# A four-layer gated model in one kernel: key constants and dispatch tables prepared beside an attention, slots in four stages, a shorter pipeline of product keys

## The chip, the core and the metric

One core of a Trainium2 chip runs the kernel. The metric is the device time of one execution in microseconds; lower is better. The engines are TensorE (PE: matmuls and transposes; its weight loads appear as PEld), VectorE (DVE), ScalarE (ACT), GpSimd (POOL), and SyncE (SP), which here only issues DMA transfers. Each engine works through its own list of instructions in order.

## The reference

Sixteen blocks of 128 tokens with 256 features pass through four layers. Each layer adds a gated cross-attention to a context and a gated feed-forward part:

```python
for l in range(4):
    x = x + tanh(g_xattn[l]) * attention[l](layernorm(x), ctx, ctx)
    x = x + tanh(g_ffn[l]) * ffn[l](layernorm(x))
# ffn[0]: top-1 of 8 experts; ffn[1]: top-2 of 8 experts and a shared one
# ffn[2]: soft mixture, 64 experts of 32 slots
logits = (x @ phi_w.T + phi_b).reshape(t, z, 64, 32)
D, C = softmax(logits, axis=3), softmax(logits, axis=2)
X = clip(einsum('tznp,tzd->npd', D, x), -33000, 65000)
Y = tanh(layernorm(X)) @ expert_w + expert_b
y = einsum('tznp,npH->tzH', C, Y)
# ffn[3]: product keys, 8 heads, two halves of 32 keys
q = batchnorm(x @ Wq + bq)              # over all tokens
s0, s1 = l2norm(q[..., :32]) @ l2norm(sub_key0).T, l2norm(q[..., 32:]) @ l2norm(sub_key1).T
# top 4 of each half, softmax over the 16 sums as weights w on experts idx
y = (gelu(expert_down[idx] @ x) * w) @ expert_up[idx]
```

## The kernel before

The residual x stays in SBUF as 16 tiles of 128 by 256. The stages run one after the other: attention 0, its experts, attention 1, its experts (routing, the shared expert, then sorted blocks), attention 2, the soft mixture (dispatch, slots, combine), attention 3, the product keys. Weights come through a pool `wp` of four large slots; normalised and transposed activations through `xtp` of four; PSUM has eight banks, each handed out by `bank`. Blocks under `manual_schedule` keep the order in which the code issues them on the named engines; elsewhere a scheduler orders the instructions when the kernel is built. In both cases each engine's order is fixed before the run, and SP's queue issues its transfers in order. A tile that takes space which a closed pool held waits until the old tiles' users, DMAs included, are done.

The experts end with POOL's scatter of each block's rows to `results` in DRAM (L974). Attention 2 (`xattn16`, L417) clears the gaps of three value tiles (L434), makes the keys of all four groups in its opening (`keys`, L442, 32 matmuls at L448, ACT adds the bias into `kraw` at L451), fetches the scattered rows (`fetch`, L508: `got`) and adds them to x (`add_gated`, L265), normalises and transposes x (L200 to L247), projects queries (L467) and values (L493), and then goes block by block: scores (L538), maxima, exponentials (L572), sums, transposes (L591), values, output. Near its end each block is normalised once more for the feed-forward part (`k`, `xnT`). An argument `draining`, used by another layer, is called in each step t.

The soft mixture, `attention_ffn2` (L1231), loads `phi` and its bias `phib`. `dispatch(u)` (L1378) handles block b and half hf, u = hf*16 + b, 1024 of the 2048 slots: four matmuls into two banks (L1386), bias added by DVE (`lg`, L1389), spilled to DRAM for the combine (L1390), maximum over the 32 slots of an expert (`red`, L1393), subtraction (L1396), exponential (ACT, L1397), maximum over experts (`top`, L1398), sum (L1400), reciprocal (L1401), and the multiply of d by POOL (L1402). `gather` (L1405) multiplies d with the normalised block into accumulators (L1412), two steps behind. After the first half, the slots 0 to 3 (groups of eight experts) run inside the second half's steps, each in three stages three steps apart in start: gather with norm (transposes, clip, statistics, `rs` on POOL by L200 and L201, `nm` on DVE at L1286, tanh on ACT at L1288), turn (transposes at L1297), expert (matmuls at L1308, with `ew` weights). Slots 4 to 7 come behind the last step, in an order written out by hand with the first shifts (L1348), sums (L1359 to L1362) and scalings (L1366 to L1369) of the combine. The combine then turns each block's weights and multiplies with the slots' outputs (L1492).

The product keys, `attention_ffn3` (L1521), start with the constants: `par` and `key` are loaded (L1528), POOL builds `havg`, `blk`, `half` and clears `kd` (L1532 to L1557), DVE squares and sums the keys, `inv_norm` (L1545) takes the power on POOL, then DVE's max and reciprocal, four scalings into the block-diagonal `kd` (L1560), and PE turns it to `kdT` (L1563). In the order as built these fall among the last slots, and the turn of kd just before attention 3's keys (L293). After attention 3 the queries' mean and variance over all tokens are taken; ACT does the gelu rows (`activations`, L1613); then a software pipeline over blocks runs stages with lags: square, norms and products, root, `exps` (L1703), `best_four` (sixteen MAX8 at L1711 and MATCH_REPLACE8 at L1715), `weigh` (L1720 to L1738; the product `pr` on POOL), `mix` (PE, L1751 and L1755), weight (L1760), turn, project (L1771), leave.

## Time and profile before

| what | us |
|---|---|
| runs of the kernel before | 1973.61, 1974.9, 1976.91 |
| median | 1974.9 |
| the profiled execution | 1977.58 |
| its span in the profile | 1975.9 |

The stages lie in that span about like this (from the timeline, by the first and last instruction of each):

| stage | from | to |
|---|---|---|
| attention 0 and experts 0 | 0 | 369 |
| attention 1 and experts 1 | 369 | 862 |
| attention 2 | 862 | 1021 |
| dispatch, with slots 0 to 3 | 1021 | 1274 |
| slots 4 to 7 | 1274 | 1306 |
| combine | 1306 | 1451 |
| attention 3 | 1451 | 1792 |
| product keys | 1792 | 1976 |

A timeline line gives start, busy time, engine, line of the code, operation, output<-inputs, shapes and how often; in brackets the idle time of that engine before it and what ended it. PE's order is fixed, so a bracket on a PE line tells what the whole engine stood waiting for. All times are of one profiled execution.

### The profile page before, as it was taken

To read this page: it belongs to the slowest core of one execution; us is meant where nothing else is said; L and a number is where in the kernel's file an instruction comes from. 1 tells how busy PE (TensorE), PEld (TensorE's weight loads), DVE (VectorE), ACT (ScalarE), POOL (GpSimd) and SP (SyncE) were. 2 spreads that over 40 slices of the span, in tenths; PEclk is the share of its full clock that TensorE was granted. 3 is DMA by queue.
4 is the path that set the end of the run, shared out by engine and by line. 5 is a ranking of instruction groups with operands and counts; after the bars stand their busy time and mean duration, and the time that the engine had idled before them with its cause. 6 is when DMAs were issued, how large, how long until landed. Compare 5 with 4: busy or idle time off the path is not lost.

```text
span 1975.9 us, 31036 instructions
## 1 busy us (share of the span) xinstructions
PE 1824.1 (92%) x10345; PEld 1219.4 (62%) x10345; DVE 1250.5 (63%) x3715; ACT 924.7 (47%) x3047; POOL 807.7 (41%) x972
## 2 busy tenths in 40 slices
PE   7996999978889999999989989889999999999897
PEld 4774566556646666656754434368866777775776
DVE  4885222389762222249969999989927667673797
ACT  5993222399931222239951121244524434443874
POOL 5873332377510454448832222211002222230796
PEclk9997999999999999999999999989999999999899
DMA  5002787510000788861012424543200000000000
GB/s 168 15 18 90 287 300 276 160 34 26 18 23 26 264 315 318 304 201 34 2 45 84 185 102 170 203 175 128 86 1 1 1 1 1 23 1 1 7 17 22
DMA packets 53138, 204.21 MB, mean 103 GB/s; under 512 B 11760, under 2 KB 31728, under 8 KB 42224
## 3 DMA queue, kind: packets, MB, share of 16 engines
q0 software_dynamic: 13584, 117.32, 16.3%
q1 hardware_dynamic: 38752, 84.87, 12.2%
q8 instruction: 84, 1.38, 0.3%
q14 instruction: 78, 0.64, 0.1%
q10 hardware_dynamic: 640, 0.00, 0.0%
HBM read 171.75 MB, written 30.41 MB: 102 GB/s over the span
## 4 chain that ended last, share of the span: by engine, by line
PE 39%; DVE 17%; ACT 4%; issue 3%; POOL 2%; DMA 2%; POOLq 0%; SPq 0%; ACTq 0%; DVEq 0%
PE pg L938 6%; PE po L1492 4%; PE pd L969 3%; PE pk L293 3%; PE pq L305 3%; PE po L388 3%; PE pv L316 3%; ACT e L572 2%; DVE rep L1715 2%; PE av L378 2%; PE sc L335 2%; DVE d L1396 2%; DVE tot L1400 1%; DVE red L1393 1%; PE pe L364 1%
## 5 line engine op out<-in xcount | busy, mean ns | idle before, releaser
L938 PE MATMUL pg<-we,xT 128*128 128x512 f32 (+1 forms) x520 | 238.4, 588 | 0.6 <-ACT xT L217 0.6
L585 POOL TENSOR_TENSOR e<-e,sums 128x512 f32<-128x512 f32 x192 | 199.0, 1069 | 69.6 <-DVE sums L582 33.2
L944 DVE TENSOR_TENSOR h<-sg,pg 128x256 f32<-128x256 f32 x132 | 54.3, 411 | 226.1 <-ACT sg L943 226.1
L572 ACT ACTIVATE e<-sc,mx 128x128 f32<-128x128 f32 x512 | 181.6, 421 | 15.9 <-DVE mx L550 14.8
L943 ACT ACTIVATE sg<-pg 128x256 f32<-128x256 f32 x132 | 49.7, 376 | 279.4 <-PE pg L938 278.1
L356 POOL TENSOR_TENSOR e<-e,rec 128x512 f32<-128x512 f32 x64 | 65.3, 1041 | 228.1 <-DVE rec L355 145.4
L938 PEld LDWEIGHTS pg<-we,xT 128*128 128x128 f32 x520 | 94.3, 193 | 78.8 <-issue 70.6
L904 POOL DMA_INDIRECT we<-in_we,rows x54 | 51.8, 958 | 213.7 <-PE pd L969 151.7
L572 ACT ACTIVATION_READ_ACCUMULATOR e<-sc,mx 128x1 f32 x512 | 133.1, 260 | 0.0
L1402 POOL TENSOR_TENSOR d<-d,tot 128x1024 f32<-128x1024 f32 x32 | 62.7, 1959 | 169.9 <-DVE tot L1401 153.2
L1412 PE MATMUL acc<-d,k 128*128 128x512 f32 x256 | 122.4, 620 | 9.5 <-POOL d L1402 9.3
L591 PE MATMUL pe<-ident,e 128*128 128x128 f32 x768 | 104.2, 278 | 28.6 <-DVE mx L555 14.2
L969 PE MATMUL pd<-we,hT 128*128 128x256 f32 x520 | 125.3, 383 | 1.2 <-ACT hT L958 1.2
L1397 ACT ACTIVATE d<-d 128x1024 f32<-128x1024 f32 x32 | 33.8, 1057 | 195.6 <-DVE d L1396 183.1
L969 PEld LDWEIGHTS pd<-we,hT 128*128 128x128 f32 x520 | 96.9, 190 | 39.2 <-issue 22.9
L1492 PE MATMUL po<-yt,cT 128*128 128x256 f32 x512 | 120.9, 380 | 0.0
L1386 PE MATMUL pl<-phi,xnT 128*128 128x512 f32 x256 | 117.5, 604 | 0.0
L200 POOL TENSOR_SCALAR ve<-mv 128x1 f32<-128x1 f32 (+1 forms) x136 | 30.5, 225 | 208.6 <-DVE mv L207 174.4
L591 PEld LDWEIGHTS pe<-ident,e 128*128 128x128 f32 x768 | 85.7, 141 | 47.4 <-POOL e L585 24.1
L572 ACT ACTIVATE e<-e,mx 128x128 f32<-128x128 f32 x256 | 99.2, 402 | 1.2 <-DVE mx L555 1.2
L1492 PEld LDWEIGHTS po<-yt,cT 128*128 128x128 f32 x512 | 92.4, 190 | 10.1
L1412 PEld LDWEIGHTS acc<-d,k 128*128 128x128 f32 x256 | 48.8, 198 | 73.1 <-issue 53.5
(315 smaller groups left out, 4360.9 us busy)
## 6 DMA issues: line engine op xcount, KB each, us to landing
spill<-lg SPq DMA_DIRECT2D x32, 512.0 KB, 3.0
ew<-in_ew SPq DMA_DIRECT2D x8, 2048.0 KB, 10.0
cw<-spill SPq DMA_DIRECT2D x14, 1024.0 KB, 8.3
got<-results SPq DMA_DIRECT2D x48, 128.0 KB, 2.1
normed<-xn SPq DMA_DIRECT2D x32, 128.0 KB, 1.7
aw<-in_aw SPq DMA_DIRECT2D x6, 512.0 KB, 3.8
ws<-in_we SPq DMA_DIRECT2D x2, 1536.0 KB, 6.6
we<-in_we SPq DMA_DIRECT2D x1, 2176.0 KB
```

What stands on the lines that cost most here:

```text
L293: nc.tensor.matmul(pk, lhsT=wk[:, k, c * P : (c + 1) * P], rhs=ctxT[g][:, k, :], start=(k == 0), stop=(k == 1))
L305: nc.tensor.matmul(pq[:, i * gt : (i + 1) * gt], lhsT=wq[:, k, (c + i) * P : (c + i + 1) * P], rhs=xnTs[g][:, k, :], start=(k == 0), stop= ...
L356: nc.gpsimd.tensor_tensor(e, e, rec.unsqueeze(2).to_broadcast([P, 4, S]), ALU.mult)
L572: nc.scalar.activation(e[:, c, :], sc[:, c, :], AF.Exp, bias=mx[:, h : h + 1], scale=sign, accum_out=sums[b][:, h : h + 1],)
L585: nc.gpsimd.tensor_tensor(e, e, r, ALU.mult)
L591: nc.tensor.transpose(pe[:, c * P : (c + 1) * P], e[:, c, :], ident)
L938: nc.tensor.matmul(pg[:, 0 : 2 * m].rearrange("p (g i) -> p g i", g=2), lhsT=tokens[j][:, k, :], rhs=wgu[:, k, :, i0 : i0 + m], start=(k = ...
L969: nc.tensor.matmul(pd[:, 0:D], lhsT=hT[0:m, ic, :], rhs=wd[0:m, ic, :], start=(ic == 0), stop=(ic == nic - 1))
L1386: nc.tensor.matmul(pl, lhsT=xnT[b // 4][:, k, tok], rhs=phi[:, k, n], start=(k == 0), stop=(k == 1))
L1402: nc.gpsimd.tensor_tensor(dv, dv, tot.unsqueeze(2).to_broadcast([P, 32, 32]), ALU.mult)
L1412: nc.tensor.matmul(acc[hf][k][q], lhsT=keep[b][:, k * P : (k + 1) * P], rhs=d[:, q * 512 : (q + 1) * 512], start=(b == 0), stop=(b == B - 1),)
L1492: nc.tensor.matmul(pos[b][:, 0:D], lhsT=cT[:, c, :], rhs=yt[2 * q + c // 2][:, c % 2, :], start=(q == 0 and c == 0), stop=(q == 3 and c == 3),
```

## The change

Seven edits, in the order of the code.

1. The constants of the product keys move, unchanged, into a function that is called at the start of the soft mixture, ahead of attention 2; their pool stays open to the end.
2. `phi` and `phib` are loaded into two of the four weight slots during attention 2 (step 2), and the first dispatch step's logits are issued in its step 21, in the tail. `phib` loses its own tile.
3. The slots in the loop have four stages, one step apart (gather, squash, turn, expert), with four `xs` buffers. As the tables hold two weight slots, expert weights are loaded two ahead and then one behind each expert; the last three are issued at the dispatch's end.
4. In the last dispatch step the multiply of d is DVE's, and `top` comes behind it.
5. The last slots are in another order; the shift and the exponentials of combine block 2 move a few steps back into the combine.
6. The product keys' stages have smaller lags, with `exps` last in a step, four gelu rows a step, and one step fewer in all. The last block's product is split between POOL (3 of 8 heads) and DVE.
7. The mask bias of attention 3 uses the `row` pool's tiles.

```diff
+def key_constants():
+    pkc = ctx.enter_context(tc.tile_pool(name="pkc", bufs=1))
+    par = pkc.tile([P, 6], F32, name="par")
+    nc.sync.dma_start(out=par, in_=a["par3"])
+    key = pkc.tile([P, 32], F32, name="key")
+    nc.sync.dma_start(out=key, in_=a["keys3"])
...
+    kdT = pkc.tile([P, P], F32, name="kdT")
+    pt = bank("pt")
+    nc.tensor.transpose(pt[:, 0:P], kd, ident)
+    nc.scalar.copy(kdT, pt[:, 0:P])
+    return par, havg, blk, kdT
...
+        constants = key_constants()
         kept = es.enter_context(ExitStack())
         kp = kept.enter_context(tc.tile_pool(name="keep", bufs=1))
         keep = [kp.tile([P, D], F32, tag=f"k{b}", name=f"k{b}") for b in range(B)]
         norm, xnT = norm_stage(keep)
-        attention2((norm, None, None, None), joining)
+        tables, first = [], {}
+        def logits(u, q):
+            hf, b = divmod(u, B)
+            n = slice(hf * 1024 + q * 512, hf * 1024 + (q + 1) * 512)
+            pl = bank("pl")
+            for k in range(2):
+                nc.tensor.matmul(
+                    pl, lhsT=xnT[b // 4][:, k, (b % 4) * S : (b % 4 + 1) * S], rhs=tables[0][:, k, n],
+                    start=(k == 0), stop=(k == 1),
+                )
+            return pl
+        def draining(t):
+            if t == 2:
+                t = load_slot(a["phi"], 4096, "phi")
+                tables.append(t[:, 0:4096].rearrange("p (c n) -> p c n", c=2))
+                pb = wp.tile([P, WSLOT], F32, tag="w", name="phib")[:, 0:2048]
+                nc.sync.dma_start(out=pb, in_=broadcast(a["phib"], 2048))
+                tables.append(pb)
+            if t == B + 5:
+                for q in range(2):
+                    first[q] = logits(0, q)
+        attention2((norm, None, None, None), joining, draining)
+        pb = tables[1]
         yp = es.enter_context(tc.tile_pool(name="soft", bufs=1))
-        pb = yp.tile([P, 2048], F32, name="phib")
-        nc.sync.dma_start(out=pb, in_=broadcast(a["phib"], 2048))
-        phi = load_slot(a["phi"], 4096, "phi")[:, 0:4096].rearrange("p (c n) -> p c n", c=2)
...
         def slots_gather(n, dp):
-            if 0 < n < 6:
-                load_experts(n + 2)
...
-            t = dp.tile([P, 2, D], F32, tag="xs", name="xs", bufs=2)
+            t = dp.tile([P, 2, D], F32, tag="xs", name="xs", bufs=4)
...
-        def slots_norm(n, dp):
-            slots_gather(n, dp)
-            slots_squash(n, dp)
-        slots = (slots_norm, slots_turn, slots_expert)
+        slots = (slots_gather, slots_squash, slots_turn, slots_expert)
...
             def dispatch(u):
                 hf, b = divmod(u, B)
                 lg = dp.tile([P, 1024], F32, tag="lg", name="lg", bufs=2)
-                tok = slice((b % 4) * S, (b % 4 + 1) * S)
                 for q in range(2):
                     n = slice(hf * 1024 + q * 512, hf * 1024 + (q + 1) * 512)
-                    pl = bank("pl")
-                    for k in range(2):
-                        nc.tensor.matmul(
-                            pl, lhsT=xnT[b // 4][:, k, tok], rhs=phi[:, k, n], start=(k == 0), stop=(k == 1)
-                        )
+                    pl = first.pop(q) if u == 0 else logits(u, q)
...
-                nc.vector.tensor_reduce(top[:, b, hf, :], lv.rearrange("t n p -> t p n"), AX.X, ALU.max)
+                if u < 2 * B - 1:
+                    nc.vector.tensor_reduce(top[:, b, hf, :], lv.rearrange("t n p -> t p n"), AX.X, ALU.max)
                 tot = dp.tile([P, 32], F32, tag="tot", name="tot")
                 nc.vector.tensor_reduce(tot, dv, AX.X, ALU.add)
                 nc.vector.reciprocal(tot, tot)
-                nc.gpsimd.tensor_tensor(dv, dv, tot.unsqueeze(2).to_broadcast([P, 32, 32]), ALU.mult)
+                if u < 2 * B - 1:
+                    nc.gpsimd.tensor_tensor(dv, dv, tot.unsqueeze(2).to_broadcast([P, 32, 32]), ALU.mult)
+                else:
+                    nc.vector.tensor_tensor(dv, dv, tot.unsqueeze(2).to_broadcast([P, 32, 32]), ALU.mult)
+                    nc.vector.tensor_reduce(top[:, b, hf, :], lv.rearrange("t n p -> t p n"), AX.X, ALU.max)
...
-                    if t in (12, 13, 14):
-                        load_experts(t - 12)
-                    n, i = divmod(t - B - 2, 3)
-                    if 0 <= n < 4:
-                        slots[i](n, dp)
+                    if t in (12, 14):
+                        load_experts((t - 12) // 2)
+                    for i, stage in enumerate(slots):
+                        n, late = divmod(t - B - 2 - i, 3)
+                        if late == 0 and 0 <= n < 4:
+                            stage(n, dp)
                     if t >= 2:
                         gather(t - 2)
+                    n, late = divmod(t - B - 6, 3)
+                    if late == 0 and 0 <= n < 3:
+                        load_experts(n + 2)
...
                 dispatch(2 * B - 1)
+                load_experts(5)
                 fetch_early(1)
+                load_experts(6)
+                load_experts(7)
                 gather(2 * B - 3)
                 gather(2 * B - 2)
...
                 combine_sum(0, dp)
-                for n in (4, 5):
-                    slots_gather(n, dp)
-                for n in (4, 5):
-                    slots_squash(n, dp)
-                combine_scale(0)
+                slots_gather(4, dp)
+                slots_gather(5, dp)
+                slots_squash(4, dp)
+                slots_gather(6, dp)
+                slots_squash(5, dp)
                 slots_turn(4, dp)
-                slots_gather(6, dp)
+                slots_gather(7, dp)
+                slots_squash(6, dp)
                 slots_turn(5, dp)
-                slots_gather(7, dp)
                 slots_expert(4, dp)
                 fetch(1)
-                for n in (6, 7):
-                    slots_squash(n, dp)
+                slots_squash(7, dp)
+                slots_turn(6, dp)
+                combine_scale(0)
                 slots_expert(5, dp)
-                for n in (6, 7):
-                    slots_turn(n, dp)
-                for n in (6, 7):
-                    slots_expert(n, dp)
+                slots_turn(7, dp)
+                slots_expert(6, dp)
+                slots_expert(7, dp)
...
+                    if u == 4:
+                        for i in range(3):
+                            combine_exp(2, i)
                     if q == 0 and b + 1 < B:
                         combine_exp(b + 1, 3)
-                    if q > 0 and b + 2 < B:
+                    if q > 0 and 0 < b < B - 2:
                         combine_exp(b + 2, q - 1)
                     if 0 <= u - 2 < 4 * B:
                         spread(u - 2)
-                    if q == 0 and b + 2 < B:
+                    if q == 0 and 0 < b < B - 2:
                         combine_shift(b + 2)
                     if q == 1 and b + 1 < B:
                         combine_sum(b + 1, cp)
                     if q == 2 and b + 1 < B:
                         combine_scale(b + 1)
+                    if u == 3:
+                        combine_shift(2)
...
+def attention_ffn3(constants):
     norm, xnT = norm_stage()
     with ExitStack() as es:
+        par, havg, blk, kdT = constants
         cp = es.enter_context(tc.tile_pool(name="pkc", bufs=1))
-        par = cp.tile([P, 6], F32, name="par")
...
-        activations(7)
...
-            rn = norms.pop(b)
+            rn, sc = norms.pop(b), raw.pop(b)
             w = pp.tile([P, 16, 32], F32, tag="wgt", name="wgt")
             for h in range(16):
-                nc.scalar.activation(w[:, h, :], raw[b][:, h, 0:32], AF.Exp, scale=rn[:, h : h + 1])
-            found[b] = w
+                nc.scalar.activation(w[:, h, :], sc[:, h, 0:32], AF.Exp, scale=rn[:, h : h + 1])
+            found[b] = w, replaced.pop(b)
         def best_four(b):
-            sc = raw.pop(b)
+            sc = raw[b]
...
-                pr, w0.unsqueeze(3).to_broadcast([P, 8, 8, 32]),
-                wv[:, :, 1, :].unsqueeze(2).to_broadcast([P, 8, 8, 32]), ALU.mult,
-            )
+            for engine, h in ((nc.gpsimd, slice(0, 8)),) if b < B - 1 else (
+                (nc.gpsimd, slice(0, 3)), (nc.vector, slice(3, 8))
+            ):
+                n = h.stop - h.start
+                engine.tensor_tensor(
+                    pr[:, h], w0[:, h].unsqueeze(3).to_broadcast([P, n, 8, 32]),
+                    wv[:, h, 1, :].unsqueeze(2).to_broadcast([P, n, 8, 32]), ALU.mult,
+                )
...
-            (2, root), (6, weight), (3, exps), (7, leave), (4, weigh), (1, norm_sums), (1, products),
-            (6, turn), (3, best_four), (5, mix), (6, project), (0, square),
+            (2, root), (5, weight), (6, leave), (3, weigh), (1, norm_sums), (1, products),
+            (5, turn), (2, best_four), (4, mix), (5, project), (0, square), (2, exps),
         )
-        for t in range(B + 7):
-            activations(min(B, 7 + 3 * (t + 1)))
+        for t in range(B + 6):
             for lag, stage in stages:
+                if stage == exps:
+                    activations(min(B, 4 + 4 * (t + 1)))
...
-            mf = rp.tile([P, S], F32, tag="mf", name="mf", bufs=2)
+            mf = row.tile([P, D], F32, tag="xn", name="mf")[:, 0:S]
...
-def attention2(after, joining):
+def attention2(after, joining, draining):
     load_attention(2)
-    xattn16(2, after=after, joining=joining)
-attention_ffn2(attention_ffn1(attention_ffn0()))
-attention_ffn3()
+    xattn16(2, after=after, joining=joining, draining=draining)
+attention_ffn3(attention_ffn2(attention_ffn1(attention_ffn0())))
```

In the first block the middle, left out, is the code of L1531 to L1560 as it was. The order as built: kdT's transpose stands on PE between the experts' last matmuls (L969) and attention 2's keys (L448); on DVE the key work stands among the first additions of `got`; on POOL the memsets, selects and the power stand behind the last scatter (L974), mixed with the value tiles' memsets; on SP's queue, phi's load (with no change of place), then par and key, then the first reads of `got`, with phib between two of them. In the dispatch's second half DVE's order around a slot becomes aggregate, reciprocal, one lg addition, `nm`, where it was aggregate, `nm`, reciprocal for slots 1 to 3.

## The prediction

> **What bounds the kernel now.** The page's busy shares come first: TensorE (PE) looks like the limit, but the share is a mean over stages, and the chain that ended last gives DVE 17% as well. So I read the stages that the change touches, each in the answer for stretches of time (columns: length, then busy time and instruction count of PE, PEld, DVE, ACT, POOL, then granted clock, DMA share, GB/s).
>
> ```profile
> PE 1824.1 (92%) x10345; PEld 1219.4 (62%) x10345; DVE 1250.5 (63%) x3715; ACT 924.7 (47%) x3047; POOL 807.7 (41%) x972
> PE 39%; DVE 17%; ACT 4%; issue 3%; POOL 2%; DMA 2%; POOLq 0%; SPq 0%; ACTq 0%; DVEq 0%
> ```
> ```profile
> 900.00:1000.00 100.00, 95.42 (x972) 73.80 (x973) 90.90 (x192) 95.62 (x467) 84.08 (x112) 1.00 0.05 15
> 1050.00:1250.00 200.00, 192.29 (x543) 83.97 (x541) 183.55 (x209) 36.15 (x42) 54.07 (x34) 0.98 0.39 149
> 1510.00:1760.00 250.00, 250.00 (x1638) 179.82 (x1638) 170.24 (x366) 104.41 (x193) 65.55 (x91) 1.00 0.02 5
> 1850.00:1950.00 100.00, 90.37 (x498) 77.66 (x498) 95.38 (x732) 75.02 (x281) 94.19 (x51) 0.97 0.05 16
> ```
>
> Attention 2 (second 900 to 1000) has PE and ACT both at 95 of 100: nothing there can win back a late start. The dispatch (1050 to 1250) goes at DVE's pace, 7.27 us a step. Attention 3 is PE without a gap. The product keys (1850 to 1950) run at 7.7 us a block with DVE and POOL both full. So at each border a late start is carried to the end, and so is an early one.
>
> **Key constants ahead of attention 2's keys: +14.5 us (10.7 to 17).** The instruction order of the changed kernel puts the transpose of the scaled keys (kdT) on PE behind the last down-projections of the experts and ahead of the 32 matmuls of attention 2's keys (L448). In the timeline of before these 32 start with no gap:
>
> ```profile
> 861.69 13.90 PE L448 MATMUL pk<-ctxT,aw 128*128 128x512 f32 x32
> 862.59 0.97 POOL L974 DMA_INDIRECT results<-y,target  x1 [1.20 <-DVE y L973]
> 869.74 0.49 POOL L434 MEMSET v<- 128x128 f32 x3 [6.18 <-DMA results<-y,target]
> 871.99 0.48 DVE L265 SCALAR_TENSOR_TENSOR x<-got,wt,x 128x256 f32<-128x256 f32 x1 [9.68 <-DMA got<-results]
> 876.22 0.41 PE L243 MATMUL pt<-ident,xn 128*128 128x128 f32 x2 [0.63 <-DVE xn L232]
> ```
>
> The experts' last scattered row block, issued at 862.59, lands at about 869.65; the v memsets wait for it because their space was the experts'. The matmuls covered that wait. In the changed kernel the new tiles (par, key, havg, kd) take space from the same closed pools, so their loads and memsets can't start before 869.7, and everything on the way to kdT comes after: key is issued behind par on SP's queue at about 870.1 and lands 1.8 us later (the key load's time to landing in before), 871.9; k2 and its sum are two DVE instructions of 0.17, 872.3; the power on POOL stands behind the memsets and selects of havg, blk, kd (2.2 us, the block at 1282.2 to 1284.4 in before) and three v memsets of 0.17, so at 872.5, 0.6 long; max and reciprocal 0.15 each, between them two L265 of 0.48 whose rows have arrived; four scalings of 0.23 to 0.26: 875.6; PE's transpose 0.27, plus semaphores: the key matmuls start at about 876.2 instead of 861.69. That is 14.5 us in which PE stands.
>
> Behind the waiting transpose stand the key matmuls, then the transposes of x, the queries, and the first scores at 882.01. Two corrections. PE was idle 6.3 of the 30 us from 870 to 900 (a ramp that waits for normed rows); the rows will be ready during the stall: from the end of the key matmuls to the first scores the 6.4 us (875.6 to 882.0) shrink to the instructions themselves, about 4.7 us (two transposes 0.41, copy 0.37, queries 1.97, values 1.03, semaphores). Against that the clock: after a PE gap, instructions run at half rate for a while. At 1276.80, after 3.1 us of idle, eight acc matmuls took 5.30 us where full speed is 3.60; at 1039.93, after 4.8 us, 5.97. So +1.7 to +2.4 here, and I take 2.2: 14.5 − 1.7 + 2.2 = 15.0, rounded down to +14.5 as some ramp idle after 882 (6.3 less what lies before it, 3.8 at most) may also go. That 3.8 in full is the lower bound, 10.7; another microsecond of landing and doubled clock loss is the upper, 17. Nothing is gained in return at the old place but 0.27 us of PE (1450.6, where PE is full, so it counts): −0.4 with its semaphore.
>
> **First dispatch logits inside attention 2's tail: −5.7 us (−6 to −3).** In before the dispatch starts like this:
>
> ```profile
> 1021.42 0.66 PE L243 MATMUL pt<-ident,k 128*128 128x128 f32 x2 [2.49 <-DVE k L232]
> 1025.59 0.69 DVE L1389 TENSOR_TENSOR lg<-pl,phib 128x512 f32<-128x512 f32 x1 [4.32 <-PE pl L1386]
> 1028.30 0.69 DVE L1389 TENSOR_TENSOR lg<-pl,phib 128x512 f32<-128x512 f32 x1 [2.01 <-PE pl L1386]
> 1029.02 1.22 DVE L1393 TENSOR_REDUCE red<-lg 128x32 f32<-128x1024 f32 x1
> ```
>
> DVE, which sets the pace, waits 4.32 + 2.01 us while four matmul pairs run at half clock (0.85 us each). In the changed kernel the first four stand between the transposes of blocks 14 and 15, where PE idles (2.49 before 1021.42): from 1018.95 at 0.43 a pass, done by 1022.4. The two additions then run at 1021.35 and 1022.65 and the maximum starts at 1023.35 instead of 1029.02. If their clock is still halved they end 3 us later: −3. The tables phi and phib now land in weight slots during attention 2, at a DMA share of 0.05, with 100 us to spare. On SP's queue phib stands among the reads of results; it lands long before use.
>
> **Slots in four stages inside the loop: +3.6 us (−2.5 to +6).** Look at what a shared port does to a tiny instruction:
>
> ```profile
> 1167.97 1.91 POOL L1402 TENSOR_TENSOR d<-d,tot 128x1024 f32<-128x1024 f32 x1
> 1168.04 1.86 DVE L1286 SCALAR_TENSOR_TENSOR nm<-mv,rs 128x2 f32<-128x2 f32 x1 [0.32 <-POOL rs L201]
> ```
> ```profile
> 1195.04 0.15 DVE L1286 SCALAR_TENSOR_TENSOR nm<-mv,rs 128x2 f32<-128x2 f32 x1
> 1196.19 1.92 POOL L1402 TENSOR_TENSOR d<-d,tot 128x1024 f32<-128x1024 f32 x1 [1.72 <-DVE tot L1401]
> ```
>
> nm has two elements a partition; 0.15 us when it runs before POOL's multiply of d, 1.86 when it comes 0.07 after it. In before this happens to slot 0 only, for slots 1 to 3 the order on DVE is nm, reciprocal. In the changed order all four have the aggregate, the reciprocal, one lg addition and then nm; POOL's two small steps for rs end about 1.2 us after the aggregate, and the multiply, whose reciprocal has been done for half a microsecond, follows at once: the order of 1167. Three more blocks of 1.86 + 0.15 each on the pace-setting engine: +6.0. Against it, the first slot's step in before lost PE 6.22 us at 1170.59 (waiting for the tanh) and DVE 1.85 at 1176.54, and with stages a step apart this wait goes: −2.4. Ends: no new block, −2.5; no gain at the first slot, +6.
>
> **End of the dispatch, last slots, start of the combine: +1 us (−2 to +3).** The last multiply of d goes from POOL, 2.16 us, to DVE, 1.21, and the last accumulation can start at 1275.1 instead of 1276.80. The maximum and the shift behind it come 2.7 us later on DVE; key work and the wait for the mask (1.46 at 1286.32) have left it. That about balances at the last slot's output. The shift of combine block 2 (2.29 us, in before run at 1300.76 in DVE's idle time) now stands inside the combine's DVE-bound start: up to +2.3, of which I take 1.
>
> **Product keys, one step shorter: −4.7 us (−6 to −3).** The first search of the four best starts at 1838.31 because exps and six of the gelu rows stood ahead; with three activations fewer ahead of the first square (1826.99, now 1823.25) and lag two, it starts near 1831. But its weights need the first exps, on ACT 1.28 of table load and 3.50 of work behind four activations a step: about 1840.5. From there the 7.7 us rhythm puts the fourth search at 1857.9 instead of 1861.83: −3.9. At the end:
>
> ```profile
> 1961.92 3.63 POOL L1738 TENSOR_TENSOR pr<-w,wgt 128x2048 f32<-128x2048 f32 x1 [0.25 <-DVE w L1732]
> 1965.61 3.29 PE L1751 MATMUL we<-pr,ident 128*128 128x256 f32 x14 [1.34 <-POOL pr L1738]
> ```
>
> The last product is split 3 to 5 between POOL and DVE. Beside each other they would take the longer, about 1.5 (1280 elements at the 1.21 per 1024 of a DVE product). But the multiply on POOL at 1268.04 (1.91) held the DVE subtraction at 1269.08 to 1.95 where the median is 1.21, that is until after its own end; so one after the other, 3/8 of 3.63 plus 1.5 = 2.8, a gain of 0.8.
>
> On this split the Trainium skill ("SBUF — State Buffer", "SBUF: two separate sides") speaks against the change: a DVE instruction with two SBUF inputs and a GpSimd one lock each other out for the whole of an instruction. By that rule this term is −4.7, beside each other −6.
>
> **Sum.** 14.5 − 0.4 − 5.7 + 3.6 + 1 − 4.7 = +8.3. The profiled span is 1975.9, its run 1977.58 (1.7 around the span), and that run lies 2.7 above the median of 1974.9; so 1974.9 + 8.3 = **1983.2**. Each term at its end gives −5 and +20; not all fall on one side, and the likeliest case's own range is 1979 to 1987.
>
> **Rivals.** (1) PE isn't held: par and key come into space that is free at 860, the constants are ready before 861.7, and the first term is 0. Then 8.3 − 14.5 = −6.2: 1968.7, faster; it decides from a stall below 2.3 us. Against it: the v memsets, in the same region, waited for the results in before, and par's load stands behind those waits. 10%. (2) The locks don't come: rs is done a little earlier and nm slips in before the multiply. Slots −2.4 instead of +3.6, total +2.3: 1977.2, no change. For it: 0.07 us decided at 1168. 20%. (3) The shorter product-key pipeline starves: weigh waits for exps that now stand last in ACT's step. In before one exps (1865.64, 3.50 long) ends 5.6 us before its weigh (1874.77); it may move back by ACT's other work, 2.9 us a step, so 2.7 are left; if the delay is 3.2 more, DVE waits 0.5 in each of 14 steps: +7, 1990.2. 15%. Forecast 55%.
>
> **Range and chances.** What this kernel's measurement can tell from no change is about 0.2%, 3.9 us. Case 1 lies on the faster side, case 2 within, the rest slower: 0.10, 0.20, 0.70. 1975 to 1991 holds the forecast, case 2 and case 3, and leaves out case 1 and some of the tails.
>
> **What would show it.** A PE gap of about 14 us ahead of L448's matmuls, ended by DVE's scaling of kd, with the first matmuls at half rate; first lg addition of the dispatch directly behind the last normalisation; nm four times near 2 us while POOL multiplies d; the fourth search 4 us earlier against the end of attention 3. Wrong, if L448 starts before 866, if nm stays at 0.15 three times, or if the rhythm of the product keys leaves 7.7.

## The result and the profile after

| | us |
|---|---|
| kernel before, median of 5 runs | 1974.9 (1973.61 to 1976.91) |
| changed kernel, median of 5 runs | 1985.02 (1982.43 to 1986.82) |
| ratio to before | 1.0046, 95% interval 1.0034 to 1.0057 |
| span of the profiled execution, before and after | 1975.9 and 1983.3 |

The change costs 10 us. 1983.2 was forecast, inside 1975 to 1991.

To see where, I cut both timelines at the same instructions and took the length of each stretch. The executions differ before any edit is reached (the experts of the second layer end at 861.85 and at 860.15), so lengths are compared, not times. The last column gives the range over all profiles, those of the experiments below among them, in which that stretch has the same code as in the kernel named.

| stretch | before | after | difference | forecast | other profiles |
|---|---|---|---|---|---|
| last expert matmul to attention 2's block 4 | 50.02 | 65.17 | +15.15 | +14.5 | constants late: 49.0 to 51.9; early: 62.4 to 66.7; only the transpose late (e1): 53.6 |
| block 4 to the first maximum of the dispatch | 117.15 | 111.27 | −5.88 | −5.7 | 115.6 to 115.8 without, 111.2 to 111.3 with the early logits |
| dispatch steps 0 to 16 | 116.56 | 116.98 | +0.42 | 0 | 115.9 to 117.0 for all |
| dispatch steps 16 to 31, with slots 0 to 3 | 122.23 | 126.09 | +3.86 | +3.6 | as before: 121.7 to 121.9; as after: 125.9 to 126.1 |
| last maximum to the last slot's output | 38.17 | 33.43 | −4.74 | +1, with the next | 37.9 before; 33.1 to 33.5 after |
| last slot to the combine's end | 144.96 | 146.04 | +1.08 | (see above) | 145.0 before; 146.0 to 147.2 after |
| border to attention 3 | −0.05 | −0.16 | −0.11 | −0.4 | |
| attention 3's first key matmul to the first square | 376.11 | 375.31 | −0.80 | −4.7, with the next | as before: 377.9 (e11); as after: 372.4 to 375.6 |
| first square to the end | 148.86 | 149.01 | +0.15 | (see above) | as before: 143.9 (e11); as after: 145.1 to 149.0 |
| sum | | | +9.1 | +8.3 | |

The page's first lines after (busy time, share, instructions) and two stretches of it (length, then busy time and count of PE, PEld, DVE, ACT, POOL, granted clock, DMA share, GB/s):

```profile
PE 1826.4 (92%) x10345; PEld 1220.3 (62%) x10345; DVE 1259.5 (64%) x3717; ACT 923.3 (47%) x3047; POOL 808.5 (41%) x971
```
```profile
860.00:874.00 14.00, 1.28 (x4) 0.64 (x4) 3.96 (x15) 0.27 (x1) 4.00 (x18) 0.68 0.68 238
1153.60:1279.70 126.10, 116.68 (x397) 50.63 (x395) 116.28 (x135) 24.05 (x31) 33.21 (x24) 1.00 0.39 142
```

PE's busy time is the same to 0.2%; it stands 12.7 of the 14 us from 860 to 874. DVE's busy time grows by 9 us with two instructions more: 2.7 of it are products taken over from POOL (1.23 and 1.49); most of the rest is waiting inside instructions: three more long nm, and twelve wgt products of 1.00 instead of 0.68, which more than make up for two instructions that got shorter (see the end of the dispatch). The timeline at attention 2's start after:

```profile
860.89 0.97 POOL L974 DMA_INDIRECT results<-y,target  x1 [1.68 <-DVE y L973]
867.26 0.21 POOL L1240 MEMSET havg<- 128x128 f32 x1 [5.40 <-DMA results<-y,target]
869.59 0.19 DVE L1260 TENSOR_TENSOR k<-key 128x32 f32<-128x32 f32 x1 [8.97 <-DMA key<-in_keys]
870.09 0.57 POOL L1254 TENSOR_TENSOR kn<-kn,half 128x1 f32<-128x1 f32 x1 [0.67 <-DVE kn L1262]
871.70 0.97 DVE L1268 TENSOR_SCALAR kd<-key,kn 32x32 f32<-32x32 f32 x4
872.87 0.45 PE L1271 MATMUL pt<-ident,kd 128*128 128x128 f32 x1 [12.72 <-DVE kd L1268]
873.11 16.72 PE L448 MATMUL pk<-ctxT,aw 128*128 128x512 f32 x32
```

Each link of the forecast chain is there, in its order: scatter landed, memsets and loads, key, power, scalings, transpose. Counted from the end of the experts, PE holds the key matmuls 13.1 us longer than before (14.5 forecast). The 32 matmuls take 16.72 instead of 13.90, 2.8 us lost at half clock (2.2 forecast). The dispatch's start, the third slot-cycle and the end, in the same timeline:

```profile
1032.23 3.60 PE L1292 MATMUL pl<-phi,xnT 128*128 128x512 f32 x8
1034.65 0.69 DVE L1448 TENSOR_TENSOR lg<-pl,phib 128x512 f32<-128x512 f32 x1
1036.59 1.22 DVE L1452 TENSOR_REDUCE red<-lg 128x32 f32<-128x1024 f32 x1
...
1201.38 1.91 POOL L1463 TENSOR_TENSOR d<-d,tot 128x1024 f32<-128x1024 f32 x1
1201.44 1.86 DVE L1354 SCALAR_TENSOR_TENSOR nm<-mv,rs 128x2 f32<-128x2 f32 x1 [0.26 <-POOL rs L201]
...
1968.86 1.49 DVE L1781 TENSOR_TENSOR pr<-w,wgt 128x1280 f32<-128x1280 f32 x1
1968.97 2.72 POOL L1781 TENSOR_TENSOR pr<-w,wgt 128x768 f32<-128x768 f32 x1 [0.22 <-DVE w L1770]
1973.13 3.19 PE L1794 MATMUL we<-pr,ident 128*128 128x256 f32 x14
```

The early logits run at full clock and DVE no longer waits for them. All four nm of the loop now meet POOL's multiply: 1.67, 1.86, 1.86 and 1.87 us, one of them (1.86) before. The last product's halves run one after the other: POOL's 768 elements take 2.72, as they wait for DVE's 1.49; together 2.83 us, where 2.8 was forecast and 3.63 was the time undivided.

### The profile page after: what moved, and what is told of

Same layout as the page of the kernel before. It is cut to its first block, busy times and chain, and to the rows that moved or that the text cites. A ratio compares the mean times of both kernels' runs of the same rounds, so it can differ in the third digit from the quotient of the medians.

```text
span 1983.3 us, 31041 instructions
## 1 busy us (share of the span) xinstructions
PE 1826.4 (92%) x10345; PEld 1220.3 (62%) x10345; DVE 1259.5 (64%) x3717; ACT 923.3 (47%) x3047; POOL 808.5 (41%) x971
## 5 line engine op out<-in xcount | busy, mean ns | idle before, releaser
L969 PE MATMUL pd<-we,hT 128*128 128x256 f32 x520 | 125.3, 383 | 1.2 <-ACT hT L958 1.2
L969 PEld LDWEIGHTS pd<-we,hT 128*128 128x128 f32 x520 | 96.9, 190 | 39.2 <-issue 22.9
```

Source lines behind the costliest of these rows:

```text
L969: nc.tensor.matmul(pd[:, 0:D], lhsT=hT[0:m, ic, :], rhs=wd[0:m, ic, :], start=(ic == 0), stop=(ic == nic - 1))
```

## The experiments

### The key constants: the transpose late, or all of them late

`e1_turn_late` moves only the transpose and its copy back, from `key_constants` to the start of `attention_ffn3`:

```diff
-        pt = bank("pt")
-        nc.tensor.transpose(pt[:, 0:P], kd, ident)
-        nc.scalar.copy(kdT, pt[:, 0:P])
...
+            pt = bank("pt")
+            nc.tensor.transpose(pt[:, 0:P], kd, ident)
+            nc.scalar.copy(kdT, pt[:, 0:P])
```

> The changed kernel with one thing undone: the PE transpose of kd and ACT's copy of it stand at the start of the last layer again; the key loads, memsets, DVE and POOL work stay ahead of attention 2. Theory (PE stands at the transpose until the results' scatter has landed and the key chain has run, and nothing wins that back): the trace of the changed kernel gives a hold of 13.1 us on the key matmuls, 2.8 us of half clock in them and 15.1 us by the fourth block; about 1 us of the ramp stays because DVE still does the key work before the first normalisation. So 14 us less than the changed kernel: about 1971. Rival (the late start comes from the transfers that were moved, par, key and phib ahead of the reads of results, and the transpose merely sits in it): no more than 3 us less, about 1982.

Measured 1970.27 (ratio to before 0.9978, 0.9966 to 0.9991): 14.8 less than the changed kernel. `e2_keys_back` calls the whole function in the last layer:

```diff
-            constants = key_constants()
...
+            par, havg, blk, kdT = key_constants(cp)
```

> The changed kernel with the whole of the key constants back in the last layer. Theory: 15.1 us less in attention 2, but the key work on DVE returns to the last slots, where I count 0 to 2 us for it: 1970 to 1972. Rival (the early key work pays nothing back later): 15 us less, 1970, and the span from the last accumulation to the end of the last slots as in the changed kernel (26.7 us there, 29.2 in the kernel before).

Measured 1969.34 (0.9973, 0.9962 to 0.9984). Its PE timeline at the start of attention 2:

```profile
860.31 0.81 PE L969 MATMUL pd<-we,hT 128*128 128x256 f32 x3
860.96 1.88 PE L448 MATMUL pk<-ctxT,aw 128*128 128x512 f32 x4
```

No gap. The rival of e1 falls: by the times one transpose in PE's list holds 14.8 of the 15.7 us. For e2 the rival is right and the theory's 0 to 2 us are 0: in the last slots the returned key work costs nothing, from last maximum to last output 33.2 us, against 33.4.

The two kernels differ by 0.9 us in their medians, but by 3.5 in the one profile of each (53.6 and 50.1 to block 4). There the key work on DVE brings the first normalised row 2.1 us later, counted from the end of the experts, and PE, idle for 2.89 instead of 0.75 us ahead of it, then makes the queries more slowly (e1, then e2):

```profile
875.34 0.41 PE L243 MATMUL pt<-ident,xn 128*128 128x128 f32 x2 [2.89 <-DVE xn L232]
878.16 3.35 PE L467 MATMUL pq<-xqT,aw 128*128 128x256 f32 x8 [0.51 <-ACT xqT L247]
```
```profile
875.60 0.41 PE L243 MATMUL pt<-ident,xn 128*128 128x128 f32 x2 [0.75 <-ACT kraw L451]
878.40 1.97 PE L467 MATMUL pq<-xqT,aw 128*128 128x256 f32 x8 [0.51 <-ACT xqT L247]
```

The same matmuls take 3.13 us in e9's profile, whose key constants are late, so this part comes and goes with the execution.

### nm away from DVE

```diff
-                nc.vector.scalar_tensor_tensor(nm, mv[:, :, 0], -1.0, rs, ALU.mult, ALU.mult)
...
+                nc.gpsimd.tensor_scalar(nm, mv[:, :, 0], -1.0, 1.0, ALU.mult, ALU.mult)
                 rsqrt(rs, mv[:, :, 1], 1e-5)
+                nc.gpsimd.tensor_tensor(nm, nm, rs, ALU.mult)
```

> The changed kernel with nm computed on POOL: one negation ahead of rs, one product behind it, so DVE has no nm any more. Theory (nm on DVE waits for the end of POOL's multiply of d, and DVE sets the pace): the four nm of the loop took 7.3 us in the changed kernel's trace and disappear; POOL's two instructions, about 0.7 us, delay its multiply, which has a step of room. 5 to 7 us less: about 1979, the shift of the dispatch's maximum between steps 16 and 31 falls from +3.9 to about -2. Rival (DVE's block is slack, since PE must wait for the tanh of the slot anyway): less than 2 us.

Measured 1973.96 (0.9996, 0.9984 to 1.0008), 11 less than the changed kernel. Around the same slot, POOL and DVE:

```profile
1198.58 0.71 POOL L201 TENSOR_TENSOR rs<-ve,nhalf 128x2 f32<-128x2 f32 x1
1199.36 0.20 POOL L1351 TENSOR_TENSOR nm<-nm,rs 128x2 f32<-128x2 f32 x1
1199.42 1.22 DVE L1453 TENSOR_REDUCE red<-lg 128x32 f32<-128x1024 f32 x1
1199.52 1.91 POOL L1464 TENSOR_TENSOR d<-d,tot 128x1024 f32<-128x1024 f32 x1
```

DVE goes on with its maximum while POOL multiplies. Steps 16 to 31 take 118.36 us instead of 126.09: 7.7 less, where the four nm had taken 7.3, so their whole time was on the path, and no less than the 5 to 7 us expected. In the profile another 3.6 us lie behind the first square of the product keys (145.40 for 149.01), where nothing was edited: the slower rhythm described below sets in later. So it does in e9 and e10, which also have nm on POOL (145.1 and 145.4; the nine other profiles with these stages have 147.1 to 149.0). Why stays open.

### The early logits taken away

```diff
-                if t == B + 5:
-                    for q in range(2):
-                        first[q] = logits(0, q)
```

> The changed kernel without the early logits: step 0 of the dispatch issues its four matmuls itself; the tables are still loaded during attention 2. Theory: 5.5 us more, about 1990.5, since DVE waits for the first logits at half clock again (4.3 and 2.0 us in the kernel before). Rival (the gain is the early arrival of the tables): no more than 1 us more.

Measured 1989.22 (1.0078, 1.0059 to 1.0097): 4.2 more. DVE waits for the two banks again, and block 4 to first maximum takes 115.76 instead of 111.27:

```profile
1043.11 0.69 DVE L1445 TENSOR_TENSOR lg<-pl,phib 128x512 f32<-128x512 f32 x1 [3.90 <-PE pl L1292]
1044.94 0.69 DVE L1445 TENSOR_TENSOR lg<-pl,phib 128x512 f32<-128x512 f32 x1 [1.14 <-PE pl L1292]
```

The order of the logits is the gain, not the early tables; it is 4.5 rather than 5.7, because here the half clock was shorter: three passes of 0.85 us in a row, as in e5 and e11, against six in the profile of before.

### The product keys alone

`e5_pk_only` is the kernel before with the sixth edit alone.

> The kernel before with the shorter product-key pipeline alone (stage lags, gelu rows, split of the last product). Theory (the first square starts 3.7 us earlier and the step rhythm stays): in the changed kernel's trace, taking off a spell of half clock at the end of attention 3, this part is worth 3.6 us; 1971, the first square 3.7 us earlier against the end of attention 3, and the rhythm 7.7 to 7.8 us. Rival (a weigh that waits for exps each step): slower than before, rhythm above 8.

Measured 1969.76 (0.9975, 0.9964 to 0.9986), 5.3 less than before (2.8 to 7.1 by the interval), near the −4.7 forecast. The first square comes 3.75 us earlier against attention 3 (372.36 for 376.11). Counted from the first statistic of the queries, which leaves attention 3 out, it does so in every profile: 40.08 us in before and in e11, whose product keys are those of before, and 36.3 in the twelve others. The rival falls: the rhythm is 7.4 to 7.8.

That the rhythm stays, the theory's other half, isn't shown. Blocks of before followed each other by 7.70 us in its profile, but by 7.39 in e11's, which is of the fastest of its ten runs; all profiles with the new lags, but for e8's edit, start at 7.0 to 7.4 and change to 7.76 between the fifth and the thirteenth interval. From attention 3's first key matmul to the end e5's profile takes 520.4 us and e11's 521.8, of which 1.8 lie in attention 3 (see the last experiment): against that execution e5's gains next to nothing. So how much of the 5.3 us is lag and how much rhythm stays open.

### The end of the dispatch and the last slots

`e6_last_order` puts back the order of the last slots and of combine block 2; `e7_last_pool` only the last dispatch step (multiply on POOL, maximum first; this is its diff).

```diff
+                    nc.vector.tensor_reduce(top[:, b, hf, :], lv.rearrange("t n p -> t p n"), AX.X, ALU.max)
...
+                    nc.gpsimd.tensor_tensor(dv, dv, tot.unsqueeze(2).to_broadcast([P, 32, 32]), ALU.mult)
-                        nc.vector.tensor_tensor(dv, dv, tot.unsqueeze(2).to_broadcast([P, 32, 32]), ALU.mult)
-                        nc.vector.tensor_reduce(top[:, b, hf, :], lv.rearrange("t n p -> t p n"), AX.X, ALU.max)
```

> The changed kernel with the order of the last slots, and the place of the shift and exponentials of combine block 2, as in the kernel before; the last multiply of d stays on DVE. Theory (the order itself is worth little): from the end of the last accumulation to the last slot's output the changed kernel took 0.9 us less than the kernel before, and its combine then loses 1.1 behind two shifts in a row: within 1 us of the changed kernel, 1985. Rival (the order is what made this stretch 4 us shorter than I forecast): 4 us more, 1989.

> The changed kernel with the last dispatch step as in the kernel before: the multiply of d on POOL, the maximum over experts ahead of the sum. Theory (the multiply waits for POOL's port, then PE comes out of an idle spell at half clock): the last accumulation ends about 3.9 us later against the last maximum, of which the earlier shift and sum on DVE give back up to 2.7 in the slots: 2 to 4 us more, 1987 to 1989. Rival (a balance, as I forecast: the maximum, the shift and the tree behind the multiply are as much later as the accumulation is earlier): no difference, 1985.

Measured 1983.52 (1.0043, 1.0026 to 1.0060) and 1984.48 (1.0053, 1.0036 to 1.0070): neither makes a difference. In e7 the last accumulation does end 3.2 us later, but the last slot's output comes 0.6 earlier: the balance, which I had forecast and then doubted, holds, and my theory for this run falls. In e6 the stretch to the last output is 34.7 instead of 33.4, and the combine 144.9 instead of 146.0. So neither explains the 4.7 us. `e11_mask_row` takes the last edit left there, in the kernel before:

```diff
-                mf = rp.tile([P, S], F32, tag="mf", name="mf", bufs=2)
+                mf = row.tile([P, D], F32, tag="xn", name="mf")[:, 0:S]
```

> The kernel before with the mask bias of attention 3 in the row pool's tiles alone. Theory (in the kernel before two of these conversions stand on DVE among the last slots and wait 1.46 us for their transfer): from the last maximum of the dispatch to the last slot's output 38.2 us become about 36.3, and the time falls by 1 to 2 us, which the measurement may not tell from nothing. Rival (DVE has slack there): 38.2 us stay.

Measured 1972.71 (0.9987, 0.9976 to 0.9998), 3.3 less than before. The stretch falls from 38.17 (37.90 in e5) to 35.08, by about 3 and not 1.9. That was the greatest part: two conversions of 0.2 us whose transfer DVE waited for, in the middle of the last slots' chain. In before:

```profile
1286.32 0.23 DVE L1825 TENSOR_SCALAR mf<-mk 128x128 f32<-128x128 uint8 x1 [1.46 <-DMA mk<-in_mask_k]
```

From 35.1 to e6's 34.7 is what the other edits of this stretch bring, and from there to 33.4 the order, 1.3.

How the balance of e7 comes about, DVE shows, before and then after:

```profile
1269.08 1.95 DVE L1396 TENSOR_TENSOR d<-lg,red 128x1024 f32<-128x1024 f32 x1
1275.02 6.21 DVE L1348 TENSOR_TENSOR cwe<-cwe,top 128x1024 f32<-128x1024 f32 x4
```
```profile
1280.98 1.23 DVE L1455 TENSOR_TENSOR d<-lg,red 128x1024 f32<-128x1024 f32 x1
1288.83 4.63 DVE L1412 TENSOR_TENSOR cwe<-cwe,top 128x1024 f32<-128x1024 f32 x4
```

With the multiply on POOL the first of the four shifts takes 2.81 us (before, e7, e11), with the multiply on DVE 1.23 (after, e6). The subtraction is shorter for another reason, as e7 has it at 1.23 too: in the changed kernel POOL's multiply of the step before ends ahead of it. So the tree behind the shifts starts 13.3 us behind the last maximum in before, 12.6 in e7 and 13.7 in the changed kernel.

### The lower bound on DVE

```diff
-                nc.vector.tensor_copy(rn, pn[:, 0:16])
+                nc.vector.tensor_scalar(rn, pn[:, 0:16], 1e-24, None, ALU.max)
...
-                nc.gpsimd.tensor_scalar(rn, rn, 1e-24, 1.0, ALU.max, ALU.mult)
```

> The changed kernel with the lower bound on the squared norms (rn) taken by DVE in the copy out of PSUM, instead of by POOL in an instruction of its own. Theory (POOL sets the rhythm of the product keys: 3.64 + 0.51 + 0.60 + 2.92 and 0.1 of gaps make the 7.76 us of a block, and DVE's product of rep and the weights loses 0.31 to a lock with that instruction of POOL): the rhythm falls to about 7.35, 11 to 12 blocks give 4 to 5 us, 1980.5. Rival (DVE sets it, and POOL's share is cover): no more than 1 us.

Measured 1984.93 (1.0050, 1.0033 to 1.0067): nothing, the rival. One block of the changed kernel, then one of this one (DVE and POOL in the timeline):

```profile
1935.03 1.00 DVE L1761 SCALAR_TENSOR_TENSOR wgt<-rep,wgt 128x512 f32<-128x512 f32 x1
1935.57 0.60 POOL L1724 TENSOR_SCALAR rn<-rn 128x16 f32<-128x16 f32 x1
1937.28 0.22 DVE L1770 TENSOR_TENSOR w<-wgt,both 128x64 f32<-128x64 f32 x1
```
```profile
1938.50 0.68 DVE L1760 SCALAR_TENSOR_TENSOR wgt<-rep,wgt 128x512 f32<-128x512 f32 x1
1940.33 0.51 POOL L1771 TENSOR_TENSOR far<-wgt,tot 128x192 f32<-128x192 f32 x1 [0.41 <-DVE tot L1763]
1940.42 0.50 DVE L1769 TENSOR_TENSOR w<-wgt,both 128x64 f32<-128x64 f32 x1
```

The collision at wgt is gone (1.00 to 0.68), and w now meets POOL's far (0.22 to 0.50): 7.67 us a block for 7.76. In both kernels DVE has gaps of 0.25 us in all a block; POOL's grow from 0.17 to 0.67. So DVE sets the rhythm, and what is taken off POOL brings its next instruction forward into DVE's next one with two SBUF inputs. Where nothing collides a block takes 7.39, as in most blocks of e3, e9 and e11.

### The repairs together

`e9_joint` joins e2 and e3. `e10_joint_combine` adds a change of the combine's start:

```diff
-                        if q == 0 and 0 < b < B - 2:
+                        if q == 0 and 1 < b < B - 2:
                             combine_shift(b + 2)
...
-                        if u == 3:
-                            combine_shift(2)
+                        if u in (3, 6):
+                            combine_shift(1 + u // 3)
```

(and the exponentials of block 3 behind it in the same way).

> The changed kernel with both repairs that the single runs showed: key constants back in the last layer, nm computed on POOL. Theory (the two losses lie in different stages and add): 15.7 and 7.7 us less than the changed kernel's 1985, about 1961.5, 0.7% faster than the kernel before. Rival (one stage's slack takes up the other's gain): no lower than 1967.

> The joint kernel with the shift of combine block 3 behind the scaling of block 2, so that two shifts (4.5 us) no longer stand in a row ahead of that scaling. Theory (PE's turn of block 2 waits for DVE there, 2.5 us in the changed kernel): the gap goes, of which the combine keeps about 1.1, since it is PE's from its tenth block on: 1 us less than the joint kernel. Rival (the wait moves to block 3): no difference.

Measured 1961.41 (0.9921, 0.9905 to 0.9938): 23.6 less than the changed kernel, where 23.4 was expected; the losses lie in different stages and both are gone (51.9 us to block 4, 118.3 for steps 16 to 31). The medians of the single runs, 15.7 and 11.1 less, would give 26.7; e9's six runs lie between 1955.0 and 1964.6. This kernel is 0.8% faster than the one before. The second, 1960.54 (0.9922, 0.9910 to 0.9935), is 0.9 faster, which runs so far apart can't tell from nothing, and its combine takes 148.7 us instead of 146.0. Its DVE and ACT at the place, and PE behind it:

```profile
1298.20 2.28 DVE L1411 TENSOR_TENSOR cw<-cw,top 128x2048 f32<-128x2048 f32 x1
1302.74 1.22 DVE L1422 TENSOR_TENSOR tree<-cw 128x1024 f32<-128x1024 f32 x1 [2.25 <-ACT cw L1417]
```
```profile
1300.52 2.19 ACT L1417 ACTIVATE cw<-cw 128x512 f32<-128x512 f32 x4 [2.03 <-DVE cw L1411]
```
```profile
1320.36 0.83 PE L1551 MATMUL pt<-ident,cw 128*128 128x128 f32 x4 [2.92 <-issue]
```

The second shift had stood where DVE must wait for block 2's exponentials anyway. Moved, it left PE's wait for block 2 as it was (2.49 us, 2.52 in e9), came due later, and PE then stood another 2.9 us ahead of block 3. By its combine my theory for this run fails, and the wait of the rival is there.

### The same kernel again

`e12_again` is the changed kernel without an edit.

> The changed kernel once more, for a second profile. Theory (a spell of half clock at the end of attention 3, 2.95 us in the changed kernel's profile, depends on the execution and not on the code): from attention 3's first key matmul to the first square of the product keys the profiles so far lie between 372.4 and 375.6 us with the same instructions; a new profile may fall anywhere between them, and the time stays at 1985. Rival (the changed kernel's own waits bring the spell): 375.3 again, and no profile of this kernel lower.

Measured 1986.2 (1.0057, 1.0042 to 1.0072). Attention 3 to the first square took 375.27, as in the first profile, so the rival isn't refuted. What the spell is shows beside e6, the end of attention 3 in both (changed kernel first):

```profile
1776.00:1792.00 16.00, 13.88 (x85) 10.18 (x85) 7.96 (x19) 6.39 (x13) 4.87 (x6) 0.79 0.01 1
```
```profile
1779.00:1792.00 13.00, 10.87 (x84) 8.24 (x84) 7.91 (x19) 6.58 (x13) 4.81 (x6) 1.00 0.01 1
```

The same work, at a granted clock of 0.79 in one and 1.00 in the other, behind an idle time of PE of 2.77 and 2.75 us. The Trainium skill ("TensorE: Matmul & The Clock Gate", "Part 1: The HAM clock gate") says that the gate's window runs freely, so its phase against the matmuls varies; the two profiles agree with that. The product keys don't bring the spell: e11, with those of before, has it too. Its lines, behind those of before:

```profile
1769.10 0.43 PE L378 MATMUL av<-eT,v 128*64 128x128 f32 x2 [2.62 <-ACT eT L366]
1771.10 3.29 PE L388 MATMUL po<-wvo,oT 128*128 128x256 f32 x14
```
```profile
1764.47 0.43 PE L378 MATMUL av<-eT,v 128*64 128x128 f32 x2 [2.75 <-ACT eT L366]
1766.76 4.64 PE L388 MATMUL po<-wvo,oT 128*128 128x256 f32 x14
```

With the seventh edit (the mask's tile, e11's only one) this idle time is 2.74 to 2.77 us, and ten of twelve profiles have the spell, 1.5 to 3.1 us long; without it (before and e5) it is 2.62, and neither has it. So the edit may well have a part in the spell, but two profiles without it are too few to show that.

## Why the prediction was right, step by step

- **Key constants ahead of attention 2** (+14.5): right in mechanism; e1 and e2 show 14.8 and 15.7 us by the time, the stretches 15.15, the means over all profiles 64.6 less 50.0. The parts differ and offset each other: the hold was 13.1 and not 14.5, the half clock 2.8 and not 2.2, the ramp gave back 2.1 and not 1.7, and the first four blocks took 1.3 longer, which no term had and three of the seven profiles with early constants don't show.
- **Early logits** (−5.7): right; 5.9 against the one profile of before, 4.2 to 4.5 by removal (e4). The term was worked out from a start at half clock that isn't always as long.
- **Slots and the lock** (+3.6): right; 3.9, and e3 shows that the lock itself is worth 7.7. Its two parts were both too large: +6.0 adds the 0.15 us of three nm instead of taking it off (5.1), and the four nm took 4.95 more than before; that leaves 1.1, an estimate, for the stages a step apart, and not 2.4. The page that the prediction names for the split product (first to start holds the port for the whole instruction) agrees with 1.86 against 0.15 and with that product's 2.83 us.
- **Last slots and the combine's start** (+1, bounds −2 to +3): wrong, −3.7. The step that failed is "that about balances at the last slot's output". The multiply by itself does balance (e7, 0.6 us), though not by the parts given: "the maximum and the shift behind it come 2.7 us later on DVE" left out the lock priced elsewhere, which kept the first shift at 2.81 us beside POOL's multiply, and the tree starts 1.1 later than in e7, 0.4 later than in before. What broke the balance is the mask's conversions, counted as 1.46 us that left DVE, for which e11 shows about 3, and the new order, 1.3 (e6). The combine's +1.08 was as forecast (+1).
- **Product keys** (−4.7): near by the time of e5 (−5.3), wrong for the pair of profiles (−0.7), where the spell of half clock at attention 3's end (2.9 us) hides it. That spell was in no term. The earlier start is right: the fourth search comes 4.8 us earlier against the first statistic than in before's profile (3.9 forecast). That the rhythm is 7.7 and stays so was read off one execution; e11 ran the same stages at 7.39, and the changed kernel went from 7.0 to 7.76.
- **Kd's transpose gone before attention 3** (−0.4): −0.1.

The stretches add up to +9.1, 0.8 above the forecast, because one term was 4.7 too high and another 4.0 too low; that is luck. The large term was the one that was read off the timeline link by link. The lower ends of the terms add up to −6.2, not −5. Rival 1 is refuted by the 12.72 us gap, rival 2 by four nm of 1.67 to 1.87, rival 3 by e5.

## What to carry to other kernels

Moving constants to an earlier place helps only if the place in every engine's list is free: here one transpose in PE's list, behind a power on POOL, behind memsets, behind another stage's scatter, cost 15 us, and placing it late cost 0.1. Ask of each tiny instruction on the engine that sets the pace which long instruction of another engine it can meet, and count such meetings in both directions, also where an edit takes one away. And before taking a wait for the cost, look at what the engine would wait for next: the shift that was moved in e10 had been free.

## What the runs showed of the hardware

- A DVE instruction with two SBUF inputs, of 2 elements a partition, lasts 0.15 us alone and up to 1.87 beside POOL's multiply.
- Two engines that lock each other settle into rhythms: the product keys ran at 7.39, 7.67, 7.70 and 7.76 us a block, by which pair of instructions met. The same stages ran at 7.70 in one profile (before) and at 7.39 in another (e11), and the rhythm changed within one execution (7.4 to 7.76 at the eighth interval of e5).
- After idle times of nearly equal length, 2.75 and 2.77 us, the mean granted clock was 1.00 once and 0.79 once, a difference of 2.8 us.
